# A graph layer on one core: verdict over the real groups, the MLP in two pieces, one-hots four groups ahead

## The chip, the cores and the metric

The kernel runs on one core of one Trainium2 chip. The metric is device time in microseconds (us) of one launch, lower is better. Engines are named as in the profile: PE (TensorE matmul), PEld (its weight loads), DVE (VectorE), ACT (ScalarE), POOL (GpSimd), SP (the queue that issues most DMAs); a q behind a name is that engine's sequencer.

## The reference

One layer of a graph network over N = 12,500 nodes and E = 412,500 edges, all fp32. `dst`, the receiving node of each edge, comes sorted.

```python
h   = relu(layernorm(x))                                  # x: 12500 x 128
agg = segment_sum(edge_attr_48, dst, num_segments=12500)  # 412500 x 48 -> 12500 x 48
u   = graph_globals[0]                                    # one graph: the same 64 numbers for all nodes
out = x + relu(concat([h, agg, u]) @ W1 + b1) @ W2 + b2   # hidden 256
```

## The kernel before

The kernel is two programs in a row. The **fast part** (the loop from line 487) uses that `dst` is sorted and evenly filled: 412,500 edges are cut into 179 groups of 2,304 (3 chunks of 768) and a tail of 84, and each chunk is taken to fall into a window of 32 nodes around the group's middle edge. Then a **verdict** `bad` (line 385) is loaded into a register of every engine (line 499), and under `tc.If(isbad >= 1)` (line 503) a **general part** computes the whole layer again, for any `dst`: one loop over 537 chunks (line 569), one over 125 blocks of 100 nodes (line 577).

What makes `bad` 1: `check_dst` and `tail_dst` sum how far relative indices lie below 0 or above 31 into columns of `chk`; `places` adds one number, the largest squared amount by which a group's middle node (`mids`) lies more than `SLACK` = 47 from where an even spread puts it (`cen`). `verdict` sends the largest of all through a clamp to 0..1. `mids` has NGP = 187 places for NG = 180 groups; the seven behind are filling. In the listing, the DMAs that fill `mids` (lines 392 and 395) stand ahead of the `memset` that zeroes it (line 409).

The fast part goes by steps, one step a group, written out by hand (`tc.manual_schedule`): a list `todo` says which functions are emitted at which step, ahead of that step's own work. Step g emits the load of group g+9 on SP (432 KB, 14 buffers), the functions of `todo[g]`, `aggregate(g)` (18 fp32 matmuls on PE, 36 instructions, in two column halves of the array, into bank g mod 3 of PSUM), `add(g-1)` (DVE adds the sums at a place read from `at_i` into the table `aggT`) and `onehot(g+2)` (DVE builds 18 one-hots of 32 from relative indices). Each engine works in the order in which its instructions were emitted, SP's DMA issues too.

The MLP runs over blocks of 512 nodes (24) and one of 212 at the end. Block j is due at step s = ready[j] + 3, when its last group is added. Around s stand: `load_x` (s-20), `stats` in two halves (s-7, s-6), `root` (ACT), `factors`, `plus_b2` (POOL), `normal` (ACT), `turn` (s-2, PE transposes) with `keep` (ACT), `first_h`, `first_a` and `relu` for hidden half 0 at s and for half 1 at s+1, `second` in two halves at s+3 and s+4, `result` (DVE) and `store` (SP). On PE that is five pieces of a block, each between two groups. `bias_of_globals` (step 2) needs the weights that ACT's queue loads in `load_weights`. `zero(i)` clears one sixteenth of `aggT` on POOL: slice 0 ahead of the loop, two slices a step from step 0 on. `spread_dst` turns the indices of a part of `dst` by PE transposes, through the same PSUM bank as `turn`.

Of the kernel before, what the change touches and what calls it, by code (L numbers as in the profile page):

```python
# [8 lines left out]
F32 = mybir.dt.float32  # L9
I32 = mybir.dt.int32  # L10
AF = mybir.ActivationFunctionType
OP = mybir.AluOpType
# [9 lines left out]
def kernel(  # L22
# [53 lines left out]


    blocks = []
    n0 = 0
    while N - n0 >= 4 * P:  # L80
        blocks.append((n0, P, 4))
        n0 += 4 * P
    if n0 < N:
        assert (N - n0) % 2 == 0 and N - n0 <= 2 * P
        blocks.append((n0, (N - n0) // 2, 2))
    NBL = len(blocks)
# [43 lines left out]
    with fast:  # L130
        ep = fast.enter_context(tc.tile_pool(name="edges", bufs=14))
        ohp = fast.enter_context(tc.tile_pool(name="oh", bufs=4))
        dp = fast.enter_context(tc.tile_pool(name="dst", bufs=2))
# [4 lines left out]
        ps_h = fast.enter_context(tc.tile_pool(name="ps_h", bufs=2, space=PSUM))  # L138
        ps_o = fast.enter_context(tc.tile_pool(name="ps_o", bufs=2, space=PSUM))
        one = fast.enter_context(tc.tile_pool(name="once", bufs=1))  # L140

        acc = [ps_agg.tile([P, 512], F32, name=f"ps{i}") for i in range(3)]
        NCK = 2 * len(parts) + 2
# [8 lines left out]
        edges, onehots, xs, scale, shift, xbs, ht, hids, pos, outs = ({} for _ in range(10))  # L152
        dsts = {}

# [57 lines left out]
        def aggregate(g):  # L212
            e, oh, ps = edges.pop(g), onehots.pop(g), acc[g % 3]
            k, n = (P, CG) if g < NGF else (TP, 1)
            for c in range(n):
                at = STEP * c if g < NGF else STEP
                for t in range(T):
                    h = HI * (t % 2)
                    nc.tensor.matmul(  # L219
                        ps[h:h + DE, at:at + W], e[:k, c, t * DE:(t + 1) * DE], oh[:k, c * T + t, :],  # L220
                        start=(c == 0 and t < 2), stop=(c == n - 1 and t >= T - 2), skip_group_check=True)

        def add(g):
            _, v = nc.values_load_multi_w_load_instructions(
                at_i[0:1, g:g + 1], engines=[DVE], min_val=low(g), max_val=high(g),
                skip_runtime_bounds_check_because="clamped to these on the chip")
            a, w = (0, WG) if g < NGF else (STEP, W)
            to = aggT[:K2, ds(v[0] + a, w)]
            nc.vector.tensor_tensor(to, to, acc[g % 3][:K2, a:a + w], OP.add)

# [7 lines left out]

        def stats(j, rs):
            a, m, r = blocks[j]  # L240
            if j not in scale:
                st = mp.tile([P, 4, 6], F32, name="st")
                mv = mp.tile([P, 4, 2], F32, name="mv")
                scale[j] = st, mv
            st, mv = scale[j]
            for q in rs:
                if q < r:
                    nc.vector.bn_stats(st[:m, q, :], xs[j][:m, q, :])
            for q in rs:
                if q < r:  # L250
                    nc.vector.bn_aggr(mv[:m, q, :], st[:m, q, :])

# [15 lines left out]
        def plus_b2(j):  # L268
            a, m, r = blocks[j]
            xb = mp.tile([P, 4, D], F32, name="xb", bufs=3)  # L270
            nc.gpsimd.tensor_tensor(xb[:m, :r], xs[j][:m, :r], b2_sb[:m, None, :].to_broadcast([m, r, D]), OP.add)
# [23 lines left out]

        def first_h(j, h):
            a, m, r = blocks[j]
            n = m * r
            ph = ps_h.tile([P, 512], F32, name="ph")
            nc.tensor.matmul(ph[:, :n], w1h[:, h * P:(h + 1) * P], ht[j][:, :n], start=True, stop=False)  # L300
            hids[j, h] = ph

        def first_a(j, h):
            a, m, r = blocks[j]
            n = m * r
            ph = hids[j, h]
            nc.tensor.matmul(ph[:, :n], w1a[:K2, h * P:(h + 1) * P], aggT[:K2, BEFORE + a:BEFORE + a + n],
                             start=False, stop=True)

        def relu(j, h):  # L310
            a, m, r = blocks[j]
            if h == 0:
                hids[j] = mp.tile([P, NH, 4, P], F32, name="hid")
            nc.scalar.activation(hids[j][:, h, :r, :m], hids.pop((j, h))[:, :m * r].rearrange("h (p r) -> h r p", r=r),
                                 AF.Relu, bias=bias[:, h:h + 1])

        def second(j, qs):
            a, m, r = blocks[j]
            if j not in pos:
                pos[j] = ps_o.tile([P, 4, D], F32, name="po")  # L320
            for q in qs:
                if q < r:
                    for h in range(NH):
                        nc.tensor.matmul(pos[j][:m, q], hids[j][:, h, q, :m], w2[:, h], start=(h == 0), stop=(h == NH - 1))

# [30 lines left out]
        def places():  # L356
# [30 lines left out]

        AHEAD = 9
        with tc.manual_schedule():
# [13 lines left out]
            nc.gpsimd.iota(iota, pattern=[[1, HI]], base=0, channel_multiplier=0,  # L403
                           allow_small_or_imprecise_dtypes=True)
            nc.gpsimd.memset(eps, EPS)
            nc.gpsimd.memset(over, float(1 - W))
            nc.gpsimd.iota(cen, pattern=[[SPAN, NGP // PER], [EACH, PER]], base=HALF, channel_multiplier=0,
                           allow_small_or_imprecise_dtypes=True)
            nc.gpsimd.memset(mids, 0)
            nc.gpsimd.memset(chk, 0.0)  # L410
            nc.gpsimd.memset(w1a, 0.0)
            warm = one.tile([P, 1], F32)
# [6 lines left out]
            nc.vector.tensor_copy(off, pv[:126, :1])  # L419
            ZN = 16  # L420
            zw = -(-aggT.shape[1] // ZN)
            zeros = [(z, min(z + zw, aggT.shape[1])) for z in range(0, aggT.shape[1], zw)]

            def zero(i):
                if i < len(zeros):
                    nc.gpsimd.memset(aggT[:, zeros[i][0]:zeros[i][1]], 0.0)

            zero(0)
            for g in range(3):
# [9 lines left out]
            places()  # L439
            onehot(1)  # L440
            load_weights()
# [6 lines left out]

            at_step(2, bias_of_globals)
            for i in range(1, len(parts)):  # L450
                need = parts[i][0] // CG
                s0 = max(2, need - 14)
                if i > 1:
                    at_step(max(2, need - 30), load_dst, i)
                at_step(s0 - 1 if i == 1 else s0, shift_dst, i)
                at_step(s0 + 1, spread_dst, i, 0)
# [4 lines left out]
            for i in range(1, ZN):  # L461
                at_step(i // 2, zero, i)
            for j in range(NBL):
                s = ready[j] + 3
                if j == NBL - 1:
                    s = NG + 2
                if j:
                    at_step(max(1, s - 20), load_x, j)
                at_step(s - 7, stats, j, (0, 1))
                at_step(s - 6, stats, j, (2, 3))  # L470
                at_step(s - 6, root, j)
                at_step(s - 5, factors, j)
                at_step(s - 5, plus_b2, j)
                at_step(s - 4, normal, j)
                at_step(s - 2, turn, j)
                at_step(s - 2, keep, j)
                at_step(s, first_h, j, 0)
                at_step(s, first_a, j, 0)
                at_step(s, relu, j, 0)
                at_step(s + 1, first_h, j, 1)  # L480
                at_step(s + 1, first_a, j, 1)
                at_step(s + 1, relu, j, 1)
                at_step(s + 3, second, j, (0, 1))
                at_step(s + 4, second, j, (2, 3))
                at_step(s + 5, result, j)
                at_step(s + 6, store, j)
            for g in range(max(todo) + 1):
# [6 lines left out]
                if 0 < g <= NG:  # L494
                    add(g - 1)
                if g + 2 < NG:
                    onehot(g + 2)

# [139 lines left out]
```

## Time and profile before

| | us |
|---|---|
| median of 3 runs | 5790.02 (5788.27 to 5802.1) |
| the profiled execution, its own time | 5793.29 |
| its span, first to last instruction | 5791.3 |
| PE busy in the span | 1728.0 (30%) |
| DVE busy in the span | 1069.6 (18%) |

The span is one execution on the one core; the own time holds 2.0 us outside it. Shares of the span are means over both parts, so each part has to be looked at by itself. The profile's groups of instructions go by line: lines under 500 are the fast part, lines from 512 on the general part.

### The profile page before, as it was taken

To read this page: it belongs to the slowest core of one execution; us is meant where nothing else is said; L and a number is where in the kernel's file an instruction comes from. 1 tells how busy PE (TensorE), PEld (TensorE's weight loads), DVE (VectorE), ACT (ScalarE), POOL (GpSimd) and SP (SyncE) were. 2 spreads that over 40 slices of the span, in tenths; PEclk is the share of its full clock that TensorE was granted. 3 is DMA by queue.
4 is the path that set the end of the run, shared out by engine and by line. 5 is a ranking of instruction groups with operands and counts; after the bars stand their busy time and mean duration, and the time that the engine had idled before them with its cause. 6 is when DMAs were issued, how large, how long until landed. Compare 5 with 4: busy or idle time off the path is not lost. (4 is left out here: it accounts for less than half of the span.)

```text
span 5791.3 us, 139158 instructions
## 1 busy us (share of the span) xinstructions
PE 1728.0 (30%) x15319; PEld 1342.1 (23%) x15320; DVE 1069.6 (18%) x3730; ACT 352.7 (6%) x902; POOL 58.6 (1%) x58
## 2 busy tenths in 40 slices
PE   8962222222222222222222222222223333333333
PEld 6741111111111111111111111111122222222222
DVE  6641111111111111111111111111111111111111
ACT  3320000000000000000000000000001111111111
POOL 2010000000000000000000000000000000000000
PEclk9975555555555555555555555555555555555555
DMA  9830000000000000000000000000000000000000
GB/s 287 277 109 20 20 21 20 20 20 20 20 21 20 20 20 20 20 21 21 20 20 20 20 21 21 20 20 20 20 14 8 8 8 8 8 8 8 8 8 8
DMA packets 186921, 188.97 MB, mean 33 GB/s; under 512 B 16241, under 2 KB 179625, under 8 KB 186843
## 3 DMA queue, kind: packets, MB, share of 16 engines
q1 hardware_dynamic: 185541, 187.36, 10.9%
q8 instruction: 58, 0.95, 0.1%
q10 hardware_dynamic: 1302, 0.49, 0.0%
q14 instruction: 20, 0.16, 0.0%
HBM read 175.00 MB, written 12.80 MB: 32 GB/s over the span
## 5 line engine op out<-in xcount | busy, mean ns | idle before, releaser
L564 PE MATMUL ps<-oh,e 128*48 128x64 f32 x6456 | 815.0, 316 | 3043.1 <-DVE oh L560 3043.1
L564 PEld LDWEIGHTS ps<-oh,e 128*48 128x48 f32 x6456 | 699.9, 198 | 3157.9 <-DVE oh L560 3157.9
L555 DVE TENSOR_SCALAR r<-rel 128x6 f32 x537 | 92.5, 172 | 1323.6 <-PEq L569 1322.8
L592 PE MATMUL pt<-ident,xn 100*128 100x100 f32 x125 | 53.5, 428 | 857.1 <-ACT xn L590 857.1
L560 DVE TENSOR_TENSOR oh<-iota,r 128x384 f32<-128x384 f32 x538 | 300.5, 559 | 18.4
L567 DVE TENSOR_TENSOR aggT<-aggT,ps 48x64 f32 x538 | 115.3, 214 | 902.2 <-PE ps L564 902.2
L558 DVE TENSOR_SCALAR r<-r 128x6 f32<-128x6 f32 x538 | 92.6, 172 | 1013.7 <-DMA e<-in_edge_attr_dram 1010.5
L548 ACT COPY relt<-pt 14x1 f32<-14x1 f32 x6 | 0.9, 148 | 3857.7 <-POOLq L551 3856.4
L592 PEld LDWEIGHTS pt<-ident,xn 100*128 100x128 f32 x125 | 22.7, 182 | 899.4 <-ACT xn L590 899.4
L600 PE MATMUL ph<-hT,w1h 128*128 128x100 f32 x500 | 187.2, 478 | 95.8 <-ACT hid L602 54.3
L601 PE MATMUL ph<-ag,w1a 48*128 48x100 f32 x500 | 186.6, 475 | 0.0
L219 PE MATMUL ps<-oh,e 128*48 128x32 f32 x6456 | 176.0, 212 | 16.6 <-DVE oh L207 11.1
L219 PEld LDWEIGHTS ps<-oh,e 128*48 128x48 f32 x6456 | 161.3, 128 | 63.7 <-issue 24.2
L607 DVE TENSOR_TENSOR ot<-po,xt 100x128 f32<-100x128 f32 x125 | 36.5, 292 | 731.0 <-PE po L605 731.0
L600 PEld LDWEIGHTS ph<-hT,w1h 128*128 128x128 f32 x500 | 125.2, 310 | 157.6 <-ACT hid L602 85.2
L605 PE MATMUL po<-w,hid 128*100 128x128 f32 x500 | 156.7, 469 | 0.0
L207 DVE TENSOR_TENSOR oh<-iota,rel 128x576 f32<-128x576 f32 x179 | 151.0, 844 | 2.4 <-ACT rel L182 2.2
L601 PEld LDWEIGHTS ph<-ag,w1a 48*128 48x128 f32 x500 | 124.8, 310 | 44.4 <-issue 44.4
L605 PEld LDWEIGHTS po<-w,hid 128*100 128x100 f32 x500 | 101.8, 264 | 34.5 <-issue 22.2
L602 ACT ACTIVATE hid<-ph,bias 128x100 f32<-128x100 f32 x250 | 86.0, 344 | 378.9 <-PE ph L601 378.9
L596 DVE COPY ag<-aggT 128x100 f32 x125 | 26.6, 213 | 335.1 <-PEq L577 333.6
L586 ACT ACTIVATE sc<-mv,eps 100x1 f32<-100x1 f32 x125 | 36.8, 295 | 801.9 <-DVE mv L585 801.9
(103 smaller groups left out, 892.0 us busy)
## 6 DMA issues: line engine op xcount, KB each, us to landing
e<-in_edge_attr_dram SPq DMA_DIRECT2D x179, 432.0 KB
e<-in_edge_attr_dram SPq DMA_DIRECT2D x537, 144.0 KB
xt<-in_x_dram SPq DMA_DIRECT2D x125, 50.0 KB
out_dram<-ot SPq DMA_DIRECT2D x125, 50.0 KB
xt<-in_x_dram SPq DMA_DIRECT2D x24, 256.0 KB
out_dram<-ot SPq DMA_DIRECT2D x24, 256.0 KB
di<-in_dst_dram SPq DMA_DIRECT2D x4, 384.0 KB
di<-in_dst_dram SPq DMA_DIRECT2D x4, 378.0 KB
```

The lines of the kernel that those rows point to most:

```text
L207: nc.vector.tensor_tensor(oh[:k, :n], iota[:k, None, :W].to_broadcast([k, n, W]), r[:, :, None].to_broadcast([k, n, W]), OP.is_equal)
L219: nc.tensor.matmul(ps[h:h + DE, at:at + W], e[:k, c, t * DE:(t + 1) * DE], oh[:k, c * T + t, :], start=(c == 0 and t < 2), stop=(c == n - ...
L555: nc.vector.tensor_scalar(r[:k], r_view, float(WA), None, OP.add)
L558: nc.vector.tensor_scalar(r[:k], r[:k], float(-WA), None, OP.add)
L560: nc.vector.tensor_tensor(oh[:k], iota[:k, None, :].to_broadcast([k, T, WA]), r[:k, :, None].to_broadcast([k, T, WA]), OP.is_equal)
L564: nc.tensor.matmul(ps, e[:k, t * DE:(t + 1) * DE], oh[:k, t, :], start=(t == 0), stop=(t == T - 1))
L567: nc.vector.tensor_tensor(to, to, ps, OP.add)
L592: nc.tensor.transpose(pt[:, :BA], xn[:BA], ident[:BA, :BA])
L600: nc.tensor.matmul(ph, w1h[:, h * P:(h + 1) * P], hT, start=True, stop=False)
L601: nc.tensor.matmul(ph, w1a[:DE, h * P:(h + 1) * P], ag[:DE], start=False, stop=True)
L602: nc.scalar.activation(hid[:, h], ph, AF.Relu, bias=bias[:, h:h + 1])
L605: nc.tensor.matmul(po[:BA], hid[:, h], w2[:, h], start=(h == 0), stop=(h == NH - 1))
```

## The change

- `bad`: the number from `places` is now made by a function `deviation` (step 4) over the first 180 of the 187 places, and the `memset` of `mids` goes ahead of its DMAs.
- PE: `first_h` and `first_a` of both hidden halves in one go at step s; `second` whole at s+3, with the next block's `turn` behind it in the same step. A block of at most 256 nodes keeps both halves in one PSUM bank.
- `onehot` four groups ahead (6 buffers), four PSUM banks of sums, one bank `po` less.
- `stats`, `root`, `factors`, `normal`, `plus_b2` on steps of their own, one block earlier.
- Clearing: `zero(i)` at step 11i - 10; `cen` and slice 0 ahead of the small `memset`s.
- Blocks: 212 nodes first, then 23 of 512, and two of 256 at the end with steps of their own.

```diff
@@ blocks
-    while N - n0 >= 4 * P:
-        blocks.append((n0, P, 4))
-        n0 += 4 * P
-    if n0 < N:
-        blocks.append((n0, (N - n0) // 2, 2))
+    if N % (4 * P):
+        blocks.append((0, N % (4 * P) // 2, 2))
+        n0 = N % (4 * P)
+    while n0 < N:
+        r = 4 if N - n0 > 4 * P else 2
+        blocks.append((n0, P, r))
+        n0 += r * P
@@ pools
-        ohp ... name="oh", bufs=4     ps_o ... bufs=2     acc = [... for i in range(3)]
+        ohp ... name="oh", bufs=6     ps_o ... bufs=1     acc = [... for i in range(4)]
@@ first_h, first_a, relu, second: the half no longer an argument
+        def bank(j, h):
+            n = blocks[j][1] * blocks[j][2]
+            small = n <= 256
+            if h == 0 or not small:
+                banks[j] = ps_h.tile([P, 512], F32, name="ph")
+            return n, small, banks[j][:, 256 * h * small:256 * h * small + n]
+        def first_h(j):
+            for h in range(NH):
+                n, small, ph = bank(j, h)
+                nc.tensor.matmul(ph, w1h[:, h * P:(h + 1) * P], ht[j][:, :n], start=(h == 0 or not small),
+                                 stop=False, skip_group_check=True)
+                hids[j, h] = ph
...
@@ places
+        def deviation():
             nc.vector.tensor_tensor(dev, dev, devc, OP.subtract)
             nc.vector.tensor_tensor(devc, dev, dev, OP.mult)
-            nc.vector.tensor_reduce(chk[0:1, NCK:NCK + 1], devc, AX.X, OP.max)
+            nc.vector.tensor_reduce(chk[0:1, NCK:NCK + 1], devc[:, :NG], AX.X, OP.max)
@@ start
             load_dst(0)
+            nc.gpsimd.memset(mids, 0)
...
-            nc.gpsimd.memset(mids, 0)
...
-            onehot(1)
+            for g in range(1, EARLY):          # EARLY = 4
+                onehot(g)
@@ steps
+            at_step(4, deviation)
-                s0 = max(2, need - 14)
+                s0 = max(1, need - 14)
-                at_step(i // 2, zero, i)
+                at_step(max(1, 11 * i - 10), zero, i)
+            start = [r + 3 for r in ready]
             for j in range(NBL):
+                s = start[j]
+                t = start[j - 1] + 3 if j else s - 3
+                last = NBL - j if j >= NBL - 2 else 0
+                n = start[min(j - 2, NBL - 4)] + 1 + (last == 1) if j > 1 else 1 + 2 * j
                 if j:
-                    at_step(max(1, s - 20), load_x, j)
+                    at_step(max(1, n - 10), load_x, j)
+                at_step(n, stats, j)
+                at_step(n + 1, root, j)
+                at_step(n + 1 + (j > 1), factors, j)
+                at_step(n + 2 + (j > 1), normal, j)
+                at_step(n + 4, plus_b2, j)
+                if not last:
+                    at_step(s, first_h, j)
+                    at_step(s, first_a, j)
+                    at_step(s, relu, j)
+                    at_step(s + 3, second, j)
+                    at_step(s + 5, result, j)
+                    at_step(s + 6, store, j)
+                    at_step(t, turn, j)
+                    at_step(t, keep, j)
+                else:
+                    at_step(NG - 2 - 2 * last, turn, j)
+                    at_step(NG - 2 - 2 * last, keep, j)
+                    at_step(NG - 2, first_h, j)
+                    at_step(NG + 2 - last, first_a, j)
+                    at_step(NG + 2 - last, relu, j)
+                    at_step(NG + 3 - last, second, j)
+                    at_step(NG + 4 - last, result, j)
+                    at_step(NG + 4 - last, store, j)
```

## Rows read from the trace of the kernel before

**Rows 1.** Stretches: PE, PEld, DVE, ACT, POOL busy, clock, DMA share, GB/s

```profile
0.00:20.00 20.00, 4.16 (x62) 3.72 (x65) 14.00 (x20) 4.19 (x9) 12.80 (x30) 1.00 0.85 238
20.00:100.00 80.00, 77.18 (x1647) 60.56 (x1644) 54.30 (x153) 30.04 (x57) 12.15 (x9) 1.00 0.95 304
...
200.00:300.00 100.00, 97.61 (x2117) 74.29 (x2118) 69.59 (x193) 35.45 (x67) 9.89 (x8) 1.00 0.88 285
...
364.00:5791.30 5427.30, 1390.30 (x8129) 1081.82 (x8129) 823.34 (x3069) 225.99 (x661) 7.84 (x1) 0.50 0.06 17
```

**Rows 2.** Timeline, how mids is filled: start, duration, engine, line, xcount, wait

```profile
0.79 1.26 ACTq L392 DMA_DIRECT2D mids<-in_dst_dram  x1
...
5.74 0.24 POOL L409 MEMSET mids<- 1x187 int32 x1 [2.51 <-DMA mids<-in_dst_dram]
```

**Rows 3.** Timeline, end of the fast part and entry into the general part

```profile
362.70 0.42 DVE L329 TENSOR_TENSOR ot<-po,xb 106x256 f32<-106x256 f32 x1 [1.46 <-PE po L324]
363.16 0.74 SPq L336 DMA_DIRECT2D out_dram<-ot  x2
364.80 0.36 SPq L528 DMA_DIRECT2D di<-in_dst_dram  x1
```

**Rows 4.** Timeline of PE, some 20 us of the steady stretch

```profile
183.26 1.00 PE L219 MATMUL ps<-oh,e 128*48 128x32 f32 x36
184.20 1.16 PE L324 MATMUL po<-w,hid 128*128 128x128 f32 x8
185.28 1.00 PE L219 MATMUL ps<-oh,e 128*48 128x32 f32 x36
...
186.80 1.81 PE L219 MATMUL ps<-oh,e 128*48 128x32 f32 x72
188.54 1.13 PE L300 MATMUL ph<-hT,w1h 128*128 128x512 f32 x2
...
190.46 1.00 PE L219 MATMUL ps<-oh,e 128*48 128x32 f32 x36
...
202.23 1.12 PE L300 MATMUL ph<-hT,w1h 128*128 128x512 f32 x2
```

**Rows 5.** Timeline of PE behind the last group, no group between pieces

```profile
358.68 0.53 PE L300 MATMUL ph<-hT,w1h 128*128 128x212 f32 x2
...
359.40 1.05 PE L324 MATMUL po<-w,hid 128*128 128x128 f32 x8
360.29 0.52 PE L300 MATMUL ph<-hT,w1h 128*128 128x212 f32 x2
```

**Rows 6.** Timeline of the first 23 us

```profile
6.23 9.81 POOL L426 MEMSET aggT<- 128x788 f32 x14
...
7.61 8.54 DVE L358 CAST mf<-mids 1x187 f32<-1x187 int32 x1
7.75 1.52 PEld L219 LDWEIGHTS ps<-oh,e 128*48 128x48 f32 x36 [1.40 <-DVE oh L207]
...
16.25 0.49 ACTq L346 DMA_DIRECT2D u<-L_gnn_graph_globals_dram  x1
...
19.26 1.66 PE L219 MATMUL ps<-oh,e 128*48 128x32 f32 x36 [9.86 <-DVE oh L207]
...
20.85 1.01 PE L353 MATMUL po<-u,w1u 64*128 64x1 f32 x4
...
22.76 1.71 POOL L271 TENSOR_TENSOR xb<-xt,b_sb 128x512 f32<-128x512 f32 x1 [6.71 <-DMA b_sb<-in_L_gnn_b_dram]
```

**Rows 7.** Lines of the fast part: busy us, mean ns of one, idle before, releaser

```profile
L207 DVE TENSOR_TENSOR oh<-iota,rel 128x576 f32<-128x576 f32 x179 | 151.0, 844 | 2.4 <-ACT rel L182 2.2 <-issue 0.2
```

**Rows 8.** Timeline, the last blocks of the general part and the end

```profile
5775.24 0.31 SPq L609 DMA_DIRECT2D out_dram<-ot  x1
5777.86 0.29 SPq L579 DMA_DIRECT2D xt<-in_x_dram  x1
...
5787.03 0.29 DVE L608 TENSOR_TENSOR ot<-ot,b_sb 100x128 f32<-100x128 f32 x1
```

More of the change, by code (lines that the diff above doesn't have):

```diff
@@ L79 @@
     n0 = 0
-    while N - n0 >= 4 * P:
-        blocks.append((n0, P, 4))
-        n0 += 4 * P
-    if n0 < N:
-        assert (N - n0) % 2 == 0 and N - n0 <= 2 * P
-        blocks.append((n0, (N - n0) // 2, 2))
+    if N % (4 * P):
+        assert N % (4 * P) % 2 == 0 and N % (4 * P) <= 2 * P
+        blocks.append((0, N % (4 * P) // 2, 2))
[4 more added lines that the diff above has]
+        n0 += r * P
     NBL = len(blocks)
@@ L131 @@
         ep = fast.enter_context(tc.tile_pool(name="edges", bufs=14))
-        ohp = fast.enter_context(tc.tile_pool(name="oh", bufs=4))
+        ohp = fast.enter_context(tc.tile_pool(name="oh", bufs=6))
         dp = fast.enter_context(tc.tile_pool(name="dst", bufs=2))
@@ L138 @@
         ps_h = fast.enter_context(tc.tile_pool(name="ps_h", bufs=2, space=PSUM))
-        ps_o = fast.enter_context(tc.tile_pool(name="ps_o", bufs=2, space=PSUM))
+        ps_o = fast.enter_context(tc.tile_pool(name="ps_o", bufs=1, space=PSUM))
         one = fast.enter_context(tc.tile_pool(name="once", bufs=1))
-        acc = [ps_agg.tile([P, 512], F32, name=f"ps{i}") for i in range(3)]
+        NACC = 4
+        acc = [ps_agg.tile([P, 512], F32, name=f"ps{i}") for i in range(NACC)]
         NCK = 2 * len(parts) + 2
@@ L152 @@
         edges, onehots, xs, scale, shift, xbs, ht, hids, pos, outs = ({} for _ in range(10))
-        dsts = {}
+        banks, dsts = {}, {}
         def load_dst(i):
@@ L212, in aggregate @@
         def aggregate(g):
-            e, oh, ps = edges.pop(g), onehots.pop(g), acc[g % 3]
+            e, oh, ps = edges.pop(g), onehots.pop(g), acc[g % NACC]
             k, n = (P, CG) if g < NGF else (TP, 1)
@@ L237, in load_x, with stats @@
             xs[j] = xt
-        def stats(j, rs):
+        def stats(j):
             a, m, r = blocks[j]
[L241 to L251, printed above, removed]
+            st = mp.tile([P, 4, 6], F32, name="st")
+            mv = mp.tile([P, 4, 2], F32, name="mv")
+            for q in range(r):
+                nc.vector.bn_stats(st[:m, q, :], xs[j][:m, q, :])
+            for q in range(r):
+                nc.vector.bn_aggr(mv[:m, q, :], st[:m, q, :])
+            scale[j] = st, mv
         def root(j):
@@ L269, in plus_b2 @@
             a, m, r = blocks[j]
-            xb = mp.tile([P, 4, D], F32, name="xb", bufs=3)
+            xb = mp.tile([P, 4, D], F32, name="xb", bufs=4)
             nc.gpsimd.tensor_tensor(xb[:m, :r], xs[j][:m, :r], b2_sb[:m, None, :].to_broadcast([m, r, D]), OP.add)
@@ L294, in keep @@
             ht[j] = hT
-        def first_h(j, h):
+        def bank(j, h):
[10 more added lines that the diff above has]
+                hids[j, h] = ph
@@ L297, in first_h, with first_a @@
+        def first_a(j):
             a, m, r = blocks[j]
             n = m * r
[L299 to L303, printed above, removed]
+            for h in range(NH):
+                nc.tensor.matmul(hids[j, h], w1a[:K2, h * P:(h + 1) * P], aggT[:K2, BEFORE + a:BEFORE + a + n],
+                                 start=False, stop=True, skip_group_check=True)
@@ L304, in first_a, with relu @@
+        def relu(j):
             a, m, r = blocks[j]
[L305 to L310, printed above, removed]
-            a, m, r = blocks[j]
[L312 to L324, printed above, removed]
+            hids[j] = mp.tile([P, NH, 4, P], F32, name="hid")
+            for h in range(NH):
+                nc.scalar.activation(hids[j][:, h, :r, :m], hids.pop((j, h)).rearrange("h (p r) -> h r p", r=r),
+                                     AF.Relu, bias=bias[:, h:h + 1])
@@ L326, in result, with second @@
+        def second(j):
+            a, m, r = blocks[j]
+            pos[j] = ps_o.tile([P, 4, D], F32, name="po")
+            for q in range(r):
+                for h in range(NH):
+                    nc.tensor.matmul(pos[j][:m, q], hids[j][:, h, q, :m], w2[:, h], start=(h == 0), stop=(h == NH - 1))
         def result(j):
@@ L388 @@
         AHEAD = 9
+        EARLY = 4
         with tc.manual_schedule():
             load_dst(0)
+            nc.gpsimd.memset(mids, 0)
             with nc.allow_non_contiguous_dma(reason="a number a group, once"):
@@ L404, with zero @@
                            allow_small_or_imprecise_dtypes=True)
+            nc.gpsimd.iota(cen, pattern=[[SPAN, NGP // PER], [EACH, PER]], base=HALF, channel_multiplier=0,
+                           allow_small_or_imprecise_dtypes=True)
+            ZN = 16
+            zw = -(-aggT.shape[1] // ZN)
+            def zero(i):
+                nc.gpsimd.memset(aggT[:, i * zw:min((i + 1) * zw, aggT.shape[1])], 0.0)
+            zero(0)
             nc.gpsimd.memset(eps, EPS)
             nc.gpsimd.memset(over, float(1 - W))
-            nc.gpsimd.iota(cen, pattern=[[SPAN, NGP // PER], [EACH, PER]], base=HALF, channel_multiplier=0,
-                           allow_small_or_imprecise_dtypes=True)
-            nc.gpsimd.memset(mids, 0)
+            nc.gpsimd.memset(w1a, 0.0)
             nc.gpsimd.memset(chk, 0.0)
-            nc.gpsimd.memset(w1a, 0.0)
             warm = one.tile([P, 1], F32)
@@ L419 @@
             nc.vector.tensor_copy(off, pv[:126, :1])
[L420 to L428, printed above, removed]
             for g in range(3):
@@ L467 @@
                 if j:
-                    at_step(max(1, s - 20), load_x, j)
[L469 to L486, printed above, removed]
+                    at_step(max(1, n - 10), load_x, j)
+                at_step(n, stats, j)
+                at_step(n + 1, root, j)
@@ L495 @@
                     add(g - 1)
-                if g + 2 < NG:
-                    onehot(g + 2)
+                if g + EARLY < NG:
+                    onehot(g + EARLY)
     isbad = nc.values_load(bad[0:1, 0:1], min_val=0, max_val=1,
```

7 lines of the change are left out of this document (2 added, 5 removed).

## The prediction

> **What bounds the kernel now.** I read the table of stretches first, because the page's shares are means over two programs. From 364 us to the end the stretch is 5,427.3 of the span's 5,791.3 us: PE is busy a quarter of it, the clock stands at 0.50 (1.2 GHz), the DMA engines at 0.06 [rows 1]. That is the general part. So 94% of the time hangs on one bit, and the first question is not how fast an engine is but why `bad` is 1.
>
> The timeline of the first microseconds answers it. The DMAs into `mids` are issued at 0.79 us, and POOL's `memset` of the same tile waits until they have landed and then writes zeros over all 187 places [rows 2]. From there on every group's middle node reads as 0, the deviations from `cen` go far beyond 47, and the clamp gives 1. Even with `mids` filled rightly the seven places behind the 180 real groups would hold 0 against centres of 12,600 and more. The end of the fast part shows the consequence: its last addition ends at 362.70 + 0.42 = 363.1 us, its last store goes out at 363.16, and SP issues line 528, the first load of the general part, at 364.80 [rows 3].
>
> The second question is what bounds the fast part, since that is what would be left. Between 200 and 300 us PE is busy 97.6 of 100 us at full clock (1.00, which is 2.4 GHz), DVE 70, ACT 35, the DMA engines 0.88 [rows 1]. PE sets the pace there, and the time that matters is the start-to-start time of its pieces. In the first 20 us it is busy for 4.2 us only [rows 1]: the start is a case of its own.
>
> **The verdict.** What the change makes of `bad` follows from the inputs, which the reference draws from a fixed seed. Worked out from them: over the 180 real groups the largest deviation is 33 nodes (47 allowed), the relative indices run from 2 to 30 (0 to 31 allowed), those of the tail from 14 to 16, and the seven filling places, now left out, deviate by up to 13,022. So every column of `chk` becomes 0, `bad` 0, and the general part is jumped over. It has no other output. Removed: 5,427 us.
>
> **The fast part, term by term,** against its end at 363.1 us.
>
> *Pieces on PE.* A piece of the MLP between two groups costs more than its matmuls. A group alone between two pieces takes 184.20 - 183.26 = 0.94 us; two in a row take 188.54 - 186.80 = 1.74, so the second costs 0.80 and being cut off 0.14 [rows 4]. A piece pays too: eight matmuls of `second` take 185.28 - 184.20 = 1.08 us between groups [rows 4] but 360.29 - 359.40 = 0.89 where no group stands next to them; `first_h` with `first_a` takes 190.46 - 188.54 = 1.92 for 512 columns, where 212 columns without neighbours take 359.40 - 358.68 = 0.72, which is 1.74 for 512 [rows 4, 5]. So 0.18 to 0.19 there and 0.14 on the group, 0.32 us a piece. Before there are 25 blocks x 5 = 125 pieces; I take off 6 behind the last group and some 10 that adjoin another piece, leaving 109. After there are 26 x 2, less the end's pieces and a few that adjoin, plus two single `turn`s: some 48. Saved: 61 x 0.32 = 19.5 us. Per block that is 3 x 0.32 = 0.96 of 202.23 - 188.54 = 13.69 us [rows 4], leaving 12.73. The bounds are 0, if another engine then sets the pace, and 25 us, if none adjoined before.
>
> *What must keep up.* DVE needs 70 us of 100 now, 75 at the new pace; its one-hot of 0.84 us a group [rows 7] is still under PE's mean of 1.7 a group. One-hots four ahead and a fourth bank let PE run on while DVE is held by `stats`; they cost nothing, since DVE's idle 30% hides them. The DMA engines move 285 GB/s at 0.88; the new pace asks for 285 x 13.69 / 12.73 = 306, and they did 304 over 80 us at a share of 0.95 [rows 1]. So I take them as just enough; if they stay at 285, the 19.5 are not had. One bank `po` instead of two, and `result` two steps behind `second`, leave five steps before the next `second` wants it: nothing. On SP, `store` stands behind the load for group s+15 as before and waits for `result`; the wait is no longer than it was.
>
> *The start.* The cast of `mids` takes 8.54 us on DVE while POOL clears 14 slices in 9.81, and PE, which did group 0 at 7.75, gets group 1 at 19.26 [rows 6]. With the clearing spread, POOL does two slices before it waits, DVE's chain is short and group 1 can run near 10 us. But step 2 puts `bias_of_globals` on PE before group 2, and that needs `u`, whose issue stands on ACT at 16.25; `b2`, issued right behind it, reaches POOL at 22.76, six microseconds later [rows 6]. With two to six microseconds for `u`, PE waits until 19 to 22 us, and before it did the bias at 20.85 without a wait. About 1 us is won there. Then block 0, now due at step 6, puts a chain (PE transposes, ACT copy, root, factors, normal, `turn`) in PE's way at steps 2 and 3, and `stats(1)` on DVE at step 3 waits for a load of `x` that competes with the first edges; I price this at 1 us. Value 0. Bounds: -9.9 (all the wait before 19.26) and +4 (PE at the slower matmuls of the start, 1.66 a group against 1.00, for four groups more) [rows 4, 6].
>
> The Trainium skill (page "SBUF — State Buffer", the bullet on the shared pair) says that DVE and GpSimd exclude each other for a whole instruction; the rows of the cast agree. By it the spread clearing would block DVE 14 times by 9.81/14 = 0.70 us, about 10 us in all, which DVE's idle time hides. So by the rule too the sum stays.
>
> *The end.* Before, PE does the last block's work behind the last group almost without waits. After, two half blocks go first_a, relu, second, first_a, relu, second, with PE waiting for ACT twice, 0.7 to 1 us each; both `first_h` and both `turn`s are done before. Value +1.5, bounds 0 and 3. From the last addition to the end of the span it takes 5,791.3 - 5,787.32 = 4.0 us in the general part [rows 8]; I take the same behind the last `result`. The jump over the general part: a block's loop takes 2.3 us on SP from the end of one store's issue to the next load's [rows 8]; bounds 0 (hidden behind the store's landing) and 2.3, value 1.
>
> The Trainium skill (page "Runtime: NRT & Kernel Launch", section "Instruction fetch mechanics") has a taken branch out of the fetched window wait for a fetch of its target. No row here shows a forward jump; by the rule the price would stand nearer the upper bound, 1 us more.
>
> *Sum:* 363.1 - 19.5 + 0 + 1.5 + 4.0 + 1.0 = 350.1 us of span, and 2.0 outside it as in the profiled execution: 352. That execution's 5,793.3 lies 3.3 us (0.06%) over the median of the runs, which at this length is 0.2 us. Predicted 352 us; this case's own range, from its terms' bounds without the extremes, is 345 to 359.
>
> **Rivals.** *The start is won.* If `u` lands by 12 us, PE goes on from group 1 without a stop: up to 9.9 us less, 342. Against it stands the issue at 16.25. Chance 0.12. *The pace isn't won.* If the DMA engines stay near 285 GB/s, or DVE's longer in-order chains hold PE, the period stays at 13.7 us and the end at 371; half of it gives 362. For it: a share of 0.95 to 0.98 needed. Chance 0.15. *The change doesn't do what it says:* `bad` is still 1, by a group that the inputs as I read them don't show. Then the general part comes back with its 5,427 us behind a fast part shorter by 18: 5,775, within 0.3% of before. Chance 0.03. *Slower:* the same bit, with PE waiting at start and end of each block for DVE's queue; since the general part costs the same, the sign then hangs on the fast part alone, and it turns against the change where this wait exceeds 0.8 us a block (26 x 0.8 = 21, more than the pieces give); slower by over 0.3% (17.4 us, which a measurement here can tell) from 1.5 us a block on: 5,790 + 18 = 5,808. DVE's idle 30% speaks against it. Chance 0.01.
>
> **How the numbers follow.** The forecast has 0.69. It, most of the early start and half of "the pace isn't won" lie between 340 and 366; outside stay the rest of these and the set bit, under 0.2. Faster 0.96, within 0.3% 0.03, slower 0.01.
>
> **What would show it.** Right: no row of a line behind the `If`; a span near 350; PE's eight matmuls of `first_h` and `first_a` in one row, sixteen of `second` with four transposes; 12.7 us between blocks; a DMA share of 0.92 to 0.96; the cast of `mids` under 1 us, and PE idle before the bias matmuls until `u` lands. Wrong: rows of the general part; gaps on PE ahead of groups that a DMA or a one-hot ends; blocks 13.7 us apart.

## The result and the profile after

Before 5791.35 us (median of 4 runs, 5788.27 to 5802.1), after 367.4 us (median of 4, 366.33 to 370.95): a ratio of 0.0635, 95% interval 0.0631 to 0.064. The profiled execution took 366.33 us. The sign and the size of the big step are as predicted; the time lies 15.4 us above the predicted 352 and 1.4 us above 366, the upper end of the prediction's wider range (its own range is 345 to 359). Ratios and their intervals are here and below those of fast executions alone, so a ratio can differ from the quotient of the medians, most for "start, nine buffers", where 0.0595 of 5795 is 345 us for a median of 348.0.

The page of the kernel after (span, busy time, clock in tenths over 40 slices, and one DMA queue with packets, MB and its share of 16 engines' time):

```profile
span 364.5 us, 16665 instructions
...
PE 322.7 (89%) x7198; PEld 258.2 (71%) x7199; DVE 221.1 (61%) x665; ACT 121.5 (33%) x245; POOL 50.2 (14%) x58
...
PEclk9999999999999999999999899999999999999998
...
q8 instruction: 58, 0.95, 1.1%
```

The general part is gone: the span ends at 364.5 us. Two further things are to be seen. PE, which sets the pace, is busy for 89% only. And queue q8 carried 58 packets of instructions, 0.95 MB, 16 KB each. Spread over PE's 7,198 matmuls and 7,199 weight loads that is 66 bytes an instruction; no other engine has a tenth as many, so I take q8 for PE's own instructions, a packet for one **page** of them.

The table of stretches (us, busy time of PE, PEld, DVE, ACT, POOL with counts, granted clock, DMA share, GB/s), for [rows 1]; the last two rows are a close look at one place. The clock reads 1.00 in the first row too, but the trace's first record of a clock, 1.00, begins at 34.4 us (before: 32.4), and a group takes 1.66 us until then and 1.00 from there on:

```profile
0.00:20.00 20.00, 5.07 (x80) 4.50 (x81) 9.05 (x26) 4.18 (x9) 4.42 (x18) 1.00 0.85 254
20.00:100.00 80.00, 73.05 (x1630) 59.77 (x1631) 51.33 (x157) 29.54 (x60) 15.65 (x14) 1.00 0.89 289
100.00:200.00 100.00, 95.51 (x2178) 75.64 (x2178) 65.99 (x198) 33.89 (x68) 13.53 (x12) 1.00 0.89 289
200.00:300.00 100.00, 92.68 (x2175) 74.02 (x2175) 63.45 (x190) 35.36 (x71) 12.57 (x11) 0.98 0.88 285
200.00:205.00 5.00, 3.33 (x146) 3.23 (x144) 3.14 (x7) 2.50 (x5) 0.00 (x0) 1.00 0.80 249
205.00:208.40 3.40, 3.40 (x43) 2.35 (x41) 2.62 (x10) 0.00 (x0) 1.61 (x1) 0.50 0.93 284
```

Between 200 and 300 us PE is busy for 92.7 of 100 us, where it was busy for 97.6; DVE does less, the DMA engines' share and rate are the same 0.88 and 285. So neither took PE's place as the bound, and yet PE stands still three times as long. The timeline of PE shows how, in rows that answer to [rows 4]:

```profile
185.18 2.05 PE L330 MATMUL po<-w,hid 128*128 128x128 f32 x16
187.06 0.60 PE L286 MATMUL pt<-ident,xn 128*128 128x128 f32 x4
187.59 3.74 PE L223 MATMUL ps<-oh,e 128*48 128x32 f32 x144
191.26 1.98 PE L307 MATMUL ph<-hT,w1h 128*128 128x512 f32 x4
...
199.86 3.33 PE L223 MATMUL ps<-oh,e 128*48 128x32 f32 x139
204.87 1.78 PE L223 MATMUL ps<-oh,e 128*48 128x32 f32 x41 [1.67 <-issue]
206.58 2.89 PE L307 MATMUL ph<-hT,w1h 128*128 128x512 f32 x4
```

The pieces are as ordered: sixteen matmuls of `second`, four transposes behind them, eight of the first layer. `second` whole takes 187.06 - 185.18 = 1.88 us, where two halves between groups took 2 x 1.08 = 2.16 [rows 4]. But between 203.19 and 204.87 PE waits for "issue", for nothing that the profile shows, in the middle of a group (behind 139 matmuls, three groups of 36 and 31 of the next), whose one-hots and edges are there or its first matmuls would not have run. And behind this wait `first_h` runs at half speed: the clock is 0.50 (1.2 GHz) from 205.0 to 208.4 us.

The waits of PE (us in total, times, longest) name the same releaser first:

```profile
PE ps L223 <- issue: 13.8, 14, 1.7
PE po L359 <- DMA e<-in_edge_attr_dram: 8.9, 1, 8.9
...
PE ps L223 <- DVE oh L211: 1.8, 2, 1.3
```

The DMA queues (packets, MB, share of the 16 engines) in the 1.3 us from 202.3 to 203.6:

```profile
q1 hardware_dynamic: 158, 0.21, 46.2%
q8 instruction: 1, 0.02, 5.2%
```

Within that stretch lies one packet of q8. I put the packets of q8 beside the waits; all of the longer ones end 1.2 to 1.6 us after a packet has landed:

```
PE's wait begins  wait us   q8 packet runs     PE goes on after landing
 52.98            1.32       51.80- 52.92      1.38
 81.73            1.60       80.80- 81.90      1.43
122.50            1.95      121.89-123.03      1.42
202.99            1.88      202.44-203.53      1.34
217.82            1.90      216.99-218.18      1.54
```

A wait is counted here from the start of the last matmul before it, whose modelled end lies 0.2 us later; so it is 1.88 us where the row above has 1.67. The waits also lie a whole number of pages apart, at about 126.7 matmuls with their weight loads each. Counted over all that PE's sequencer runs (matmuls, weight loads, semaphore instructions), this is exact: in the traces of all kernels here, every wait of over 0.05 us ahead of a group's matmul between 36 and 350 us, 85 in all, falls at the 193rd or 194th instruction of a run of 256, the same place each time; and 16 KB over 256 are 64 bytes an instruction, near the 66 above. For the table below I added up PE's gaps of over 0.05 us between 36 and 350 us that end 1.1 to 1.7 us after a q8 packet's landing, and call them **page stalls** (a packet lands every six us or so, so some one in ten gaps with another cause gets in). Before: 9 of 7.2 us in all. After: 22 of 18.5 us. By the modelled ends, and at that place of 256 alone, they are 9 of 6.0 us and 18 of 15.7 us.

The start, for [rows 2, 6], with the DVE row of the verdict's cast:

```profile
0.77 0.24 POOL L400 MEMSET mids<- 1x187 int32 x1 [0.29 <-POOLq L641]
1.04 1.51 ACTq L402 DMA_DIRECT2D mids<-in_dst_dram  x1
...
8.37 0.24 DVE L364 CAST mf<-mids 1x187 f32<-1x187 int32 x1
...
10.71 1.66 PE L223 MATMUL ps<-oh,e 128*48 128x32 f32 x36 [0.55 <-DVE oh L211]
...
16.62 0.54 ACTq L352 DMA_DIRECT2D u<-L_gnn_graph_globals_dram  x1
...
21.29 0.98 PE L359 MATMUL po<-u,w1u 64*128 64x1 f32 x4 [8.93 <-DMA e<-in_edge_attr_dram]
...
23.06 1.66 PE L223 MATMUL ps<-oh,e 128*48 128x32 f32 x36
```

`mids` is zeroed ahead of its DMAs, the cast takes 0.24 us where it took 8.54, group 1 starts at 10.71 instead of 19.26; then PE waits 8.93 us at the bias, whose `u` was issued at 16.62. The row puts the wait down to edges; with eleven buffers (below) the same wait has `u` itself as its releaser:

```profile
PE po L359 <- DMA u<-L_gnn_graph_globals_dram: 9.5, 1, 9.5
```

The end, for [rows 3, 5]:

```profile
357.89 1.30 PE L330 MATMUL po<-w,hid 128*128 128x128 f32 x8 [0.62 <-ACT hid L322]
...
359.28 0.42 DVE L335 TENSOR_TENSOR ot<-po,xb 128x256 f32<-128x256 f32 x1 [2.37 <-PE po L330]
359.73 0.33 SPq L342 DMA_DIRECT2D out_dram<-ot  x1
```

The last addition ends at 359.70 us (before: 363.12), the span 4.8 us later. To [rows 8] nothing answers.

### The profile page after: what moved, and what is told of

Its sections match the earlier page's. It is cut to its first block, busy times and chain, and to the rows that moved or that the text cites. A ratio compares the mean times of both kernels' runs of the same rounds, so it can differ in the third digit from the quotient of the medians.

```text
span 364.5 us, 16665 instructions
## 1 busy us (share of the span) xinstructions
PE 322.7 (89%) x7198; PEld 258.2 (71%) x7199; DVE 221.1 (61%) x665; ACT 121.5 (33%) x245; POOL 50.2 (14%) x58
## 4 chain that ended last, share of the span: by engine, by line
PE 85%; issue 5%; DMA 4%; DVE 2%; ACT 1%; SPq 1%; ACTq 0%; DVEq 0%
PE ps L223 41%; PE po L330 13%; PE ph L307 13%; PE ph L315 12%; PE pt L286 3%; PE pt L185 2%; DMA w1u<-in_L_gnn_W_dram 2%; DMA xt<-in_x_dram 1%; DMA e<-in_edge_attr_dram 1%; DVE oh L211 1%; SPq L119 0%; DVE aggT L233 0%; ACT hT L292 0%; PE po L359 0%; SPq L164 0%
## 5 line engine op out<-in xcount | busy, mean ns | idle before, releaser
L223 PEld LDWEIGHTS ps<-oh,e 128*48 128x48 f32 x6456 | 157.0, 127 | 41.4 <-issue 36.2
L223 PE MATMUL ps<-oh,e 128*48 128x32 f32 x6456 | 165.7, 212 | 15.9 <-issue 13.8
L233 DVE TENSOR_TENSOR aggT<-aggT,ps 112x80 f32 x180 | 42.2, 235 | 115.0 <-PE ps L223 104.5
L271 POOL TENSOR_TENSOR xb<-xt,b_sb 128x512 f32<-128x512 f32 (+2 forms) x26 | 36.1, 1390 | 276.1 <-DMA xt<-in_x_dram 168.0
L322 ACT ACTIVATE hid<-ph,bias 128x512 f32<-128x512 f32 (+2 forms) x52 | 34.1, 661 | 119.3 <-PE ph L315 117.9
L330 PE MATMUL po<-w,hid 128*128 128x128 f32 (+1 forms) x392 | 50.8, 282 | 1.2 <-ACT hid L322 1.2
L307 PE MATMUL ph<-hT,w1h 128*128 128x512 f32 (+2 forms) x104 | 50.4, 608 | 1.6 <-issue 1.6
L330 PEld LDWEIGHTS po<-w,hid 128*128 128x128 f32 (+1 forms) x392 | 45.8, 191 | 3.1 <-ACT hid L322 2.0
L315 PE MATMUL ph<-aggT,w1a 112*128 112x512 f32 (+2 forms) x104 | 46.7, 572 | 0.0
L278 ACT ACTIVATE xn<-xt,sh,sc 128x128 f32<-128x128 f32 (+1 forms) x98 | 40.1, 484 | 0.4 <-DVE sh L265 0.4
L307 PEld LDWEIGHTS ph<-hT,w1h 128*128 128x128 f32 x104 | 18.6, 198 | 14.6 <-issue 13.4
```

The source lines that it names most:

```text
L223: nc.tensor.matmul(ps[h:h + DE, at:at + W], e[:k, c, t * DE:(t + 1) * DE], oh[:k, c * T + t, :], start=(c == 0 and t < 2), stop=(c == n - ...
L233: nc.vector.tensor_tensor(to, to, acc[g % NACC][:K2, a:a + w], OP.add)
L278: nc.scalar.activation(xn[:m, q], xs[j][:m, q], AF.Relu, bias=shift[j][:m, q:q + 1], scale=scale[j][:m, q:q + 1])
L307: nc.tensor.matmul(ph, w1h[:, h * P:(h + 1) * P], ht[j][:, :n], start=(h == 0 or not small), stop=False, skip_group_check=True)
L315: nc.tensor.matmul(hids[j, h], w1a[:K2, h * P:(h + 1) * P], aggT[:K2, BEFORE + a:BEFORE + a + n], start=False, stop=True, skip_group_check ...
```

## The experiments

The reading to be tested: PE waits for its own instructions, because it now uses up a page faster than the next one comes through DMA engines that are busy with edge loads. The rivals: the edges or one-hots are late; the new order of pieces saves nothing; the start holds everything back. Nine kernels ran; the stalls are those of one profiled execution each, whose own time stands beside them.

| kernel | median us (range) | ratio to before, 95% | profiled us | page stalls | at a page's end, by modelled ends |
|---|---|---|---|---|---|
| after | 367.4 (366.3 to 371.0) | 0.0635, 0.0631 to 0.0640 | 366.3 | 22, 18.5 us | 18, 15.7 |
| verdict only | 368.0 (366.2 to 369.5) | 0.0636, 0.0634 to 0.0637 | 366.2 | 6, 4.0 | 5, 3.2 |
| a third of the edges | 343.8 (342.8 to 343.9) | 0.0593, 0.0591 to 0.0594 | 343.6 | 1, 0.1 | 0, 0 |
| five pieces | 370.8 (367.8 to 374.7) | 0.0639, 0.0635 to 0.0644 | 367.8 | 7, 3.7 | 4, 2.4 |
| eleven buffers | 360.2 (354.5 to 362.7) | 0.0623, 0.0619 to 0.0627 | 354.5 | 13, 11.9 | 10, 8.3 |
| nine buffers | 353.6 (351.7 to 355.0) | 0.0609, 0.0606 to 0.0612 | 354.8 | 12, 10.0 | 9, 6.7 |
| seven buffers | 354.2 (350.8 to 359.4) | 0.0609, 0.0604 to 0.0614 | 353.0 | 13, 8.8 | 9, 6.3 |
| start | 360.3 (359.6 to 362.9) | 0.0623, 0.0620 to 0.0626 | 359.6 | 17, 19.0 | 16, 15.9 |
| start, nine buffers | 348.0 (342.9 to 350.6) | 0.0595, 0.0591 to 0.0599 | 350.6 | not counted | 8, 8.9 |
| that and three pieces | 350.0 (347.7 to 350.9) | 0.0604, 0.0602 to 0.0606 | 350.0 | 9, 7.4 | 8, 6.2 |

**Verdict only.** The kernel before with two edits:

```diff
+            nc.gpsimd.memset(mids, 0)        # ahead of the DMAs into mids
...
-            nc.gpsimd.memset(mids, 0)
-            nc.vector.tensor_reduce(chk[0:1, NCK:NCK + 1], devc, AX.X, OP.max)
+            nc.vector.tensor_reduce(chk[0:1, NCK:NCK + 1], devc[:, :NG], AX.X, OP.max)
```

> The kernel before with two lines changed: the memset of the group middles ahead of their DMAs, and the deviation taken over the 180 real groups. If the general part is left out by these two lines alone, the time is the old fast part: its last addition at 363.1 us, 4.8 to the end of the span as in the changed kernel, 1.8 outside, so 369 to 371 us. Then all other edits together are worth 2 to 3 us of the 367.4. If instead the rest is worth the 18 us that were forecast, this kernel takes 385 or more; if the rest costs time, 367 or less.

368.0 us: the two edits are the whole gain, and all others together are worth 0.6 us, less than the two ranges. It lies a little under the 369 to 371 expected. Its waits of PE:

```profile
PE pt L181 <- DVE df L173: 11.0, 2, 10.7
PE ps L219 <- issue: 3.1, 4, 1.1
```

PE still waits 10.7 us at the start, but no longer behind the cast, and little for instructions:

```profile
3.65 10.22 POOL L426 MEMSET aggT<- 128x788 f32 x14
...
4.31 8.87 DVE L173 TENSOR_SCALAR df<-di,sub 30x768 f32<-30x768 int32 x1 [1.13 <-DMA di<-in_dst_dram]
...
16.05 0.24 DVE L358 CAST mf<-mids 1x187 f32<-1x187 int32 x1
```

The DVE instruction that stands beside POOL's clearing is now the subtraction of line 173: 8.87 us, where the kernel after, with the clearing spread, takes 1.35 for it. The cast, behind the clearing, takes 0.24. Its stretch from 100 to 200 us:

```profile
100.00:200.00 100.00, 99.08 (x2211) 76.79 (x2211) 72.42 (x191) 35.88 (x66) 10.19 (x8) 1.00 0.87 279
```

PE is at 99.1% here and gets through 2,211 matmuls; the kernel after, at 95.5%, gets through 2,178. The new order does its work in less time and loses it again standing still.

**A third of the edges.** The kernel after; two thirds of the edge data are not loaded, and each group multiplies its first chunk's edges three times. Each instruction of PE stays.

```diff
-                load_edges(e, g * CG, CG)
+                load_edges(e, g * CG, 1)
...
-                        ps[h:h + DE, at:at + W], e[:k, c, t * DE:(t + 1) * DE], oh[:k, c * T + t, :],
+                        ps[h:h + DE, at:at + W], e[:k, 0, t * DE:(t + 1) * DE], oh[:k, c * T + t, :],
```

> The changed kernel with only the first chunk of every group loaded (144 KB for 432) and used for all three, so two thirds of the edge data are left out and the output is not the reference's; every instruction of TensorE is the same. Theory A, TensorE waits for pages of its own instructions, whose 16 KB packets wait on the busy DMA engines: the stalls between 36 and 352 us (22 us in the changed kernel) fall under 6 us, and with the start's wait for the weights shortened the time is 335 to 347 us. Theory B, a page costs a fixed time whatever the DMA engines do: the stalls stay near 20 us, and only the start gains, 357 to 365 us. Theory C, the stalls are waits for edge data: they go too, but without instruction packets landing 1.2 to 1.6 us before each resumption in the changed kernel's trace.

343.8 us, 23.7 less. The stretch from 100 to 200 us:

```profile
100.00:200.00 100.00, 99.98 (x2359) 80.02 (x2358) 68.50 (x208) 36.30 (x70) 14.78 (x13) 1.00 0.48 141
```

PE's matmuls of the groups from 36 to 330 us (busy us, mean ns of one | idle before):

```profile
L223 PE MATMUL ps<-oh,e 128*48 128x32 f32 x6118 | 148.3, 209 | 0.0
```

With the DMA engines at 0.48 PE never stands in this stretch, and a matmul of a group takes what it took (209 ns, 210 in the kernels before and after). The mean over 20 blocks, from the first layer of the third block on, is 13.77 us before, 13.62 after, 12.64 here. Blocks in which PE never waits show the pieces alone: with eight groups in a block 13.68 us before (188.54 to 202.23) and 12.77 here (103.90 to 116.67), with seven 12.87 before (119.18 to 132.05) and 11.96 both here and after (56.66 to 68.63). So the order of pieces gives its saving, and the load on the DMA engines takes it. That it is the instructions and not the edges follows from the places of the waits, inside groups and at page boundaries; the next runs test it by kernels that move all the edge data.

The packets show where the time goes. Put in order beside the ends of PE's pages, a packet starts 2.7 us (median) behind a page's end in the kernel after and 0.6 us behind it here; it then takes as long in both, 1.09 and 1.12 us. So the edge loads delay the start of a packet, not its passage.

**Five pieces.** The kernel after, with the pieces of before:

```diff
-                    at_step(s, first_h, j)
-                    at_step(s, first_a, j)
-                    at_step(s, relu, j)
-                    at_step(s + 3, second, j)
+                    for h in range(2):
+                        at_step(s + h, first_h, j, (h,))
+                        at_step(s + h, first_a, j, (h,))
+                        at_step(s + h, relu, j, (h,))
+                    at_step(s + 3, second, j, (0, 1))
+                    at_step(s + 4, second, j, (2, 3))
...
-                    at_step(t, turn, j)
+                    at_step(t + 2 * (j > 0), turn, j)      # keep likewise
```

> The changed kernel with the MLP of a block in five pieces on TensorE again (each half of the hidden layer at a step of its own, the second layer in two halves, the transposes two steps later), all else as changed. Theory A, long runs of groups use up a page of instructions sooner than the next one lands, and pieces in between stretch it: stalls fall back to about 10 us of 22, while some 60 more pieces at 0.32 us come back, so 367.4 - 12 + 19 = 372 to 376 us. If the stalls don't depend on how the pieces lie: 384 to 388 us. If pieces cost nothing (the 0.32 us misread): 355 to 360 us.

370.8 us, just under the 372 to 376 expected, with fewer stalls than the 10 us expected. PE's passages from a group to a piece, counted from 36 to 350 us, rise from 55 to 119, which at 0.32 us is +20.5; the stalls fall by 14.8, and the stretch at 1.2 GHz (1.7 us) is gone: +4.0 expected from these, +1.5 measured between the two profiled executions that they are counted from (+3.4 between the medians). Its longest row of "issue":

```profile
PE ps L223 <- issue: 2.4, 4, 1.3
```

The same loads by the same queue with the same depth, and few stalls. The data are not late; what differs is how soon PE has used up a page. Counted from the traces between 36 and 350 us, 31 of the 54 pages after hold under 5.3 us of PE's work (one of 107 group matmuls and 20 of the MLP: 4.9; the shortest, of group matmuls alone: 2.8). All 18 waits at a page's end stand behind these 31 and none behind the 23 longer pages. With five pieces, 19 of 54 are that short. A packet also starts sooner there, 1.7 us behind a page's end for 2.7; how much each of the two is worth is not shown.

**Fewer buffers of edges.** The kernel after; eleven and seven likewise (`AHEAD` 7 and 4):

```diff
-        ep = fast.enter_context(tc.tile_pool(name="edges", bufs=14))
+        ep = fast.enter_context(tc.tile_pool(name="edges", bufs=9))
...
-        AHEAD = 9
+        AHEAD = 6
```

> The changed kernel with edges loaded 6 groups ahead into 9 buffers, for 9 ahead into 14. If an instruction packet waits behind the edge packets that are queued ahead of it, a shorter queue shortens the wait, the stalls fall to some 14 us of 22, and the time to 357 to 362 us. If it only shares the engines' bandwidth, the stalls and the time stay: 366 to 369 us. If edges land too late, new waits for them appear and the time goes over 370 us.

> The changed kernel with edges 7 groups ahead into 11 buffers, between the changed kernel (14: 367.4 us) and nine (353.6 us). If the stalls go by the depth of the queue, it lies between them, 357 to 363 us with 12 to 16 us of stalls for instruction pages. If the gain of nine came from something else that changes at one point only (the order of loads and stores on the queue), it equals one of the two.

> The changed kernel with edges 4 groups ahead into 7 buffers. Theory: the stalls for instruction pages fall with the queue ahead of them: 14 buffers 18.5 us of such stalls, 9 buffers 10.0; 7 buffers give 4 to 7 us and 347 to 351 us, unless edges then come late, which shows as TensorE waiting where no instruction packet has just landed, and over 354 us.

14, 11, 9 and 7 buffers: 18.5, 11.9, 10.0 and 8.8 us of stalls. By the medians the time follows to nine buffers, 13.8 us less than after, and not further. Nine gained more than the 357 to 362 us expected. Eleven met its time, not quite its stalls; and the profiled execution in which they were counted took 354.5 us, as little as nine's, while its others took 358 to 363, so eleven's place between is less sure than its median looks. Seven missed its expectation and stands where nine does, without waits for edges. A packet starts 1.9 to 2.0 us (median) behind a page's end with eleven, nine and seven, for 2.7 with 14. Of nine's gain 2.5 us lie at the start: the first layer of block 1 begins at 40.86 us for 43.37. The bytes are the same and the DMA engines are no less busy. With nine buffers:

```profile
100.00:200.00 100.00, 96.29 (x2201) 77.03 (x2198) 63.65 (x193) 34.57 (x67) 13.24 (x12) 0.97 0.92 286
200.00:300.00 100.00, 98.03 (x2269) 77.97 (x2270) 65.02 (x205) 35.45 (x71) 13.76 (x12) 1.00 0.97 306
```

306 GB/s at 0.97, the rate that the prediction asked for, and PE at 98%, in the second of these stretches. The profiled execution also holds a stretch of 6.8 us at clock 0.50, from 119.5 us on. So a shorter line of loads lets instructions through sooner; loading less far ahead costs nothing visible.

**Start.** The kernel after; what holds PE in the first steps is put later:

```diff
-            check_dst(0)
-            at_step(2, bias_of_globals)
+            at_step(8, bias_of_globals)
+            at_step(8, check_dst, 0)
-                s0 = max(1, need - 14)
+                s0 = max(4, need - 14)
+            start[0] = 8
...                                             # and block 0's other steps behind it
```

> The changed kernel with another order at the start alone: the bias matmuls, which wait for the weights until 21.3 us, at step 8 instead of 2, the first check of dst there too, part 1 of dst spread at steps 5 and 6, block 0 due at step 8, block 1's statistics at step 8. If those waits are what kept the start from gaining, TensorE goes on from group 1 at 10.7 us, reaches group 6 ten us earlier than the changed kernel (34.8 us there), and the time falls by 6 to 10 us to 357 to 361. If edges or another wait hold it there anyway: 365 to 368.

360.3 us, 7.1 less. PE's start:

```profile
10.70 5.38 PE L223 MATMUL ps<-oh,e 128*48 128x32 f32 x144 [0.55 <-DVE oh L211]
...
19.46 1.00 PE L223 MATMUL ps<-oh,e 128*48 128x32 f32 x36
...
22.30 0.60 PE L359 MATMUL po<-u,w1u 64*128 64x1 f32 x4
```

Groups 1 to 4 run in a row, group 6 starts at 19.46 instead of 34.77, the bias waits for nothing. Part of these 15 us is work put off: block 0's pieces and the bias now stand behind group 6. The first layer of block 1 stands behind the same 14 groups in both kernels. In the kernel after:

```profile
43.37 1.98 PE L307 MATMUL ph<-hT,w1h 128*128 128x512 f32 x4
```

and here:

```profile
34.68 2.23 PE L307 MATMUL ph<-hT,w1h 128*128 128x512 f32 x4
```

That is 8.7 us ahead, and 6.7 arrive at the end of the profiled executions: the stalls stay at 19.0, and twice more the clock stands at 0.50 for 3.4 us (at 31.8 and 59.1), of which the second costs 1.7 us behind this place.

**Both.** Start with nine buffers, and this with the first layer's halves at s and s+2 and `second` at s+4:

```diff
+                    for h in range(2):
+                        at_step(s + 2 * h, first_h, j, (h,))     # first_a, relu likewise
...
-                    at_step(s + 3, second, j)
+                    at_step(s + 4, second, j)
```

> The start of the run before it and nine edge buffers together. If the two losses are separate, both gains add: 353.6 less 6 to 10, so 343 to 348 us, ahead of every kernel here. If the faster start only brings edges late with the short prefetch: 350 to 355 us.

> The kernel with the other start and nine buffers (348.0 us), a block's MLP in three pieces set two and two and three groups apart: the two hidden halves at s and s+2, the second layer with the next block's transposes at s+4. A page of TensorE's instructions then holds a part of a piece each time and lasts longer at its shortest. If that takes most of the 10 us of stalls for pages away, it outweighs 24 more pieces at 0.32 us (7.7 us): 343 to 347 us. If nine buffers have already taken what there is to take, the pieces cost and it is 352 to 356 us.

348.0 us for both, the fastest kernel here that does the whole work, 19.4 us below the changed one and within what was expected if both gains add. Three pieces gave 350.0, between its two cases. By the ratios it is some 5 us slower (0.0604 for 0.0595, and the intervals don't meet): 77 passages instead of 55 cost 7.0 us, and the stalls at a page's end fall only from 8.9 to 6.2. That spreading can be tuned to gain more is not shown.

## Why the prediction was right and where it failed

**Right: the verdict.** `bad` is 0, nothing behind the `If` runs; 5,427 us are gone, and verdict-only shows that two lines do it.

**Right: the pieces on PE.** 116 passages before and 55 after are the 61 of the sum. The prediction's block of 13.69 us, which has eight groups and no wait, should last 12.73; with a third of the edges such a block lasts 12.77. Five pieces against two come out within 2.5 us of the 20.5 that 0.32 us each gives.

**Wrong: "What must keep up".** The step that failed is the one that takes the suppliers of PE "as just enough". It went through DVE, the DMA engines and SP as the suppliers of PE, and left one out, at a price of nothing: PE's own instructions, which come through the same DMA engines. No row shown there speaks of them, though the kernel before had 7.2 us of such stalls, and q8 stood on the profile's page. The rival nearest to it, "the pace isn't won", has the loss in the right size (blocks 13.6 us apart, where its sign was 13.7) and the wrong cause: the DMA engines did the full rate once fewer loads stood in line (306 GB/s between 200 and 300 us), and DVE held PE for 1.8 us between 36 and 350 us (before: 0.6). The last addition came at 359.70 where the sum has 345.1. From rows and counts of the profiled execution the 14.6 us are: 18.5 - 7.2 = 11.3 of page stalls; 1.7 of the stretch at half clock, which began right behind a stall; 1.0 because full clock began at 34.4 us instead of 32.4, two us at half speed; 0.6 that is left over. The 1.2 us more that DVE held PE are not among these terms, so the account closes to about a microsecond.

**Right: start, tail, end.** The start gained nothing, and PE waited for `u` as described. PE waited for ACT twice at the end, 0.56 and 0.62 us: 1.2 where 1.5 stood. From the last addition to the end 4.8 us where 5.0 stood, and 1.8 outside where 2.0 stood. That POOL's clearing would hold DVE for about 10 us does not show: in the kernel after a one-hot beside a clearing alone takes its 0.75 us; those of 1.5 to 1.7 us all stand beside POOL's addition of line 271.

The Trainium skill (page "Runtime: NRT & Kernel Launch", section "Instruction fetch mechanics") has each engine fetch 16 KB blocks of 256 instructions by a DMA queue of its own while it runs the current one, the crossing "mostly hidden". The size and the queue agree with q8's 58 packets. The hiding holds with the DMA engines at 0.48 (0.1 us of stalls) and not at 0.89 with 14 buffers (18.5 us); here the measurement decides. The same section's fetch behind a taken branch, which the prediction set at up to 1 us more, does not show in the 4.8 us of the end.

Left open: whether the instruction packet, whose start is what comes late, waits for the engine that carries it or for the order among the queues; why a packet starts no sooner with seven buffers than with nine; and what is to be had from page boundaries that fall behind dear matmuls by intent, which was not tried. What sets off the half-speed stretches is open too: those at 205.0 us (after), 59.1 and 212.7 (start) begin behind a wait of 1.7 to 2.5 us, the one at 119.5 (nine buffers) 0.5 us before the end of one of 2.7, those at 31.8 (start) and 23.5 (three pieces) behind waits of 0.81 and 0.34, those at 17.6 (10.2 us long) and 34.7 (start, nine buffers) behind waits of 1.4, and the waits of 1.95 and 1.90 us at 122.5 and 217.8 in the kernel after have none behind them.

## What to carry to other kernels

An engine with thousands of short instructions has one more supplier: count its instructions per us against the instruction queue's packets on the profile's page, and look for "issue" waits that end just behind a packet's landing and lie whole multiples of a packet's instructions apart. Making such an engine's work denser shortens the time that it has for each page, so a saving there may come back as stalls unless the bulk loads are queued less deep; a prefetch deeper than needed isn't free. And the first run to make of a change in many parts is the one part that carries it, alone.

## What was not expected of the hardware

A 16 KB packet of instructions takes about 1.1 us (202.44 to 203.53), with a third of the edge loads no less, and PE goes on only 1.2 to 1.6 us behind its landing. The edge loads delay its start: 2.7 us behind a page's end, 0.6 with a third of them. A shallower line of loads raised the bytes moved as well, 306 GB/s against 285 between 200 and 300 us, though not between 100 and 200 (286 against 289). And right behind a wait of 1.9 us the granted clock fell to 0.50 for 3.4 us with PE busy throughout, in a stretch that was otherwise at 1.00; behind other waits of that length it did not.
